# The values' product of two steps back directly behind the scores, in an attention stage that shares TensorE with experts

## The chip, the core and the metric

The kernel runs on one NeuronCore of a Trainium2 chip. Five engines work from their own instruction queues: TensorE (PE; its weight loads are listed apart as PEld), VectorE (DVE), ScalarE (ACT), GpSimd (POOL) and SyncE (SP, here only a queue that issues DMAs). They wait for each other by semaphores. The metric is device time in microseconds (us) of one execution. All data are float32.

## What is computed

The reference is a network of two layers on 8 x 512 tokens of width 256. The first layer (a state-space block and a mixture of eight experts) is not touched by the change. The second layer is an attention block plus a mixture of experts, both on the same normalised rows:

```python
xn = _layernorm(x, axis=-1)
x = x + _L1_attn_ref(xn, ...) + _L1_ffn_ref(xn, ...)

# attention: 16 heads of 16, batch 8, sequence 512
scores = jnp.einsum('bhqd,bhkd->bhqk', qh, kh) * scale
scores = scores * decay[None, None, :, :]
attn = jax.nn.softmax(scores, axis=-1)
out = jnp.einsum('bhqk,bhkd->bhqd', attn, vh)

# experts: seven experts with 512 rows each, and one that passes its rows on
h = jax.nn.relu(jnp.einsum('ceh,ehi->cei', inputs, experts_inter))   # 256 -> 1024
out = jnp.einsum('cei,eih->ceh', h, experts_out) * in_w[..., None]   # 1024 -> 256
combined = jnp.zeros_like(x_flat).at[used_idx].add(out.reshape(-1, hidden))
```

## The kernel before

All engines run the instructions in the order in which the program issues them (a schedule written by hand). The first layer takes roughly the first 1100 us. Behind it comes the loop over attention steps, in which everything named here happens.

An attention step covers one batch `b`, one group `g` of four heads and one block `c` of 128 keys, against all 512 queries: 8 x 4 x 4 = 128 steps. A step's work is spread over three rounds of the loop:

- `scores` (L1554): four matmuls, one for each head, contracting over 16 rows. The heads lie at partitions 0, 32, 64 and 96, so that the four run beside each other in four row groups of the array; each writes a bank of its own, of four (`s_ps`). VectorE multiplies each with the decay, takes the maximum and writes the result `s` (L1564), then makes `ng` and `w` from the maxima (L1569, L1571).
- one round later: `shares` (L1573, a small exponential of `w`), `exps((0, 1))` and `exps((2, 3))` (L1576: the exponentials of two heads each, in place, on ACT) and `weigh` (L1580: VectorE scales the values by `w` into `wv`).
- two rounds later: `values` (L1584): four matmuls that contract over the 128 keys and write 32 partitions each of one bank `o_ps`, so that the four run beside each other in four column groups. They need `wv` and the four exponentials. After the fourth block of keys (`c == 3`) `divide` (L1651) copies `o_ps` to `os` on ACT and stores it to DRAM by SP.

A float32 matmul is recorded as two MATMUL instructions, so that a step has eight for the scores and eight for the values.

Between these, `fill()` (L1729) issues one piece of other work on the whole 128 x 128 array. It takes the first of: a piece that is half done, urgent work, and the experts, the last only while fewer of their pieces are spent than `due()` (L1713) asks for at this step. In the first steps it takes late work of the layer before instead. The pieces of the experts come from `experts()` (L1383). For each half of an expert (256 rows) there are 17:

- one piece that transposes the rows (`e_tp`, L1399) and has ACT copy them (`e_xdT`, L1400)
- eight of the first layer (`e_hp`, L1407: four MATMUL instructions each), each followed on ACT by a ReLU (`e_hT`, L1410)
- eight of the second layer (`e_yp`, L1420: four MATMUL instructions each), in two groups of four that, once begun, go on at every `fill()`; behind the fourth of a group ACT scales the result (`e_yo`, L1426) and POOL adds it to rows in DRAM (L1427)

All of them write to two banks in turn. Urgent work is the output projection of a finished batch (`finish`, L1517: four pieces `fin`, each with a copy on ACT and an addition on VectorE), and, at the end, the last batch's own steps.

A round has up to four pieces. In what follows they are A, B, C and D: A behind `exps((0, 1))` and ahead of the values, B behind the values, then `exps((2, 3))` and `weigh`, then C and D. On TensorE only the scores, the values and the pieces appear; on ACT the exponentials stand between the pieces' own copies and ReLUs.

Of the kernel before, what the change touches and what calls it, by code (L numbers as in the profile page):

```python
# [63 lines left out]
def tile_kernel(ctx: ExitStack, tc: tile.TileContext, t, out: bass.AP):  # L64
# [505 lines left out]
    with ExitStack() as es:  # L570
# [648 lines left out]
        with tc.manual_schedule(engines=ENGINES):  # L1219
# [62 lines left out]
            def fill(n):  # L1282
                for _ in range(n):
                    if next(rows, "end") == "end":
                        next(rest, None)
# [73 lines left out]
    with tc.tile_pool(name="a1", bufs=1) as p1, tc.tile_pool(name="a2", bufs=2) as p2, tc.tile_pool(  # L1359
# [89 lines left out]
        def load_some(k):  # L1449
            for to, of in loads[:k]:  # L1450
                Y.dma_start(out=to, in_=of)
            del loads[:k]

        def inputs_of(b):
            rows, vd = kept[b]
            got = {"q": [], "k": [], "v": p2.tile([P, TPB, VW], FP, name="vt", tag="vt")}
            Y.dma_start(out=got["v"], in_=vd)
            for n in ("q", "k"):
                spread(rows[n], got[n], n)
            return got  # L1460
# [26 lines left out]
        class Ending:  # L1487
# [11 lines left out]
            def divide(self):  # L1499
                tq = psum.tile([P, 2, P], FP, name="tq", tag="s_ps", bufs=4)  # L1500
                T.transpose(tq[:, 0, :], self.os[:, self.at], ident)
                T.transpose(tq[:, 1, :], self.last, ident)
                self.oq = columns(tq)
# [188 lines left out]
        with tc.manual_schedule(engines=ENGINES):  # L1692
# [53 lines left out]
            def more():  # L1746
                if spent == WORK:
                    next(rows, None)

            def follow():  # L1750

                nonlocal work, ready, e1, e2
                if late_left:
                    pass
                elif ready is None:
                    ready = n
                    tls.close()
                    e1 = es.enter_context(tc.tile_pool(name="f1", bufs=1, side="right"))
                    e2 = es.enter_context(tc.tile_pool(name="f2", bufs=2, side="right"))
                    work = experts()  # L1760
                    next(work)
                elif n == ready + 1:
                    next(work)

            def own_rows(b):
                Y.dma_start(out=x_sb[:, b * TPB : (b + 1) * TPB, :], in_=rows_of(xn1, b))
# [4 lines left out]
            for n in range(N + 2):  # L1771

                if n < N:
                    b, g, c = steps[n]
                    if (g, c) == (2, 0) and b + 1 < B:
                        got = inputs_of(b + 1)
                    if (g, c) == (1, 0) and b < B - 1:
                        own_rows(b)
                        if b == B - 2:
                            own_rows(B - 1)  # L1780
                    if b == B - 1 and g == 0:
                        xi = x_sb[:, b * TPB + c, :]
                        V.tensor_scalar(xi, xi, noop[:, b * TPB + c : b * TPB + c + 1], None, ALU.mult)
                    if (g, c) == (0, 0):
                        now_in = got
                        od = dram.tile([4, 4, 32, S], FP, name="od", tag="od", bufs=2)
                        rd = dram.tile([AH, S], FP, name="rd", tag="rd", bufs=2)
                        scratch = (od, rd, [])
                    now = Step(b, g, c, now_in)
                    now.scratch = scratch  # L1790
                    done.append(now)
                    now.scores()
                load_some(6)
                for chain in list(chains):
                    if next(chain, "end") == "end":
                        chains.remove(chain)
                if ready is not None and n == ready + 3:
                    idle.append(work)
                last = done[n - 1] if 1 <= n <= N else None
                if last:  # L1800
                    last.shares()
                    last.exps((0, 1))
                    fill()
                m = n - 2
                if m >= 0:
                    s = done[m]
                    if s.c == 0:
                        s_op = psum.tile([P, S], FP, name="o_ps", tag="o_ps", bufs=2)
                    s.values(s_op)
                    if s.c == TPB - 1:  # L1810
                        if m == N - 1:
                            tails = [Ending(s.b, c, s_op, s.scratch[2]) for c in range(TPB)]
                        else:
                            chains.append(divide(s.b, s.g, s_op, *s.scratch))
                            next(chains[-1], None)
                if last:
                    fill() or more()
                    last.exps((2, 3))
                    last.weigh()
                    fill()  # L1820
                    fill() or more()
                    if late_left:
                        fill()
                follow()
# [77 lines left out]
def build(arrays):  # L1902
    import concourse.bacc as bacc

    nc = bacc.Bacc("TRN2", target_bir_lowering=False, num_devices=1)
    t = {
        k: nc.dram_tensor(f"in_{k}_dram", v.shape, mybir.dt.from_np(v.dtype), kind="ExternalInput").ap()
        for k, v in arrays.items()
    }
    out = nc.dram_tensor("out_0_dram", (NT, DM), FP, kind="ExternalOutput").ap()  # L1910
    with tile.TileContext(nc) as tc:
        tile_kernel(tc, t, out)
    return nc
# [10 lines left out]
```

## Time and profile before

| | |
|---|---|
| three runs, median (lowest to highest) | 1805.91 us (1796.79 to 1808.62) |
| the profiled execution | 1802.12 us, its span 1800.4 us |
| mean granted TensorE clock in the span | 0.913 of full speed |
| first scores, last values of the attention steps | 1137 us, 1784 us from the span's start |
| first and last piece of the experts' first layer | 1212 us, 1714 us |

The profile's page gives for each engine its busy time, and the groups of instructions with their idle time and what ended it. The ends of matmuls are modelled, so TensorE can be listed as busy while it waits; the distance from one start to the next tells more. In a timeline the columns are the start (us from the span's start), the duration from the first to the last instruction of the line (us), engine, line of the program, operation, what is written and read, shapes, and how many instructions are merged; in brackets the idle time before and what ended it.

### The profile page before, as it was taken

The page shows a single profiled execution, that of the slowest core. Times are in us where ns is not written, and L with a number is a line of the kernel's source. Part 1 is how long each engine was busy: PE and PEld are TensorE (multiplying, and loading weights), DVE is VectorE, ACT ScalarE, POOL GpSimd, SP SyncE. Part 2 cuts the span into 40 slices and gives each one's busy share as a digit, 9 for nine tenths or more (in the row PEclk, how much of TensorE's full clock was granted, in tenths as well). Part 3 has the DMA queues.
Part 4 walks back from the last instruction along what each step waited for, and adds up shares of the span by engine and source line. Part 5 has one row for each costly group of instructions (what it writes and reads, how often), then busy time and mean ns, then how long its engine had stood idle before and what let it go on. Part 6 is the DMA issues. An engine that isn't in the chain of part 4 may idle for free.

```text
span 1800.4 us, 25907 instructions
## 1 busy us (share of the span) xinstructions
PE 1630.7 (91%) x8736; PEld 980.5 (54%) x8736; DVE 1201.4 (67%) x3166; ACT 914.8 (51%) x2173; POOL 574.7 (32%) x520
## 2 busy tenths in 40 slices
PE   6556889989999999998798889879999999999997
PEld 6224567667677776775455556444544545444442
DVE  6578586575765765757877575566667666666674
ACT  4232344454454544544544523337767676766674
POOL 0041465475574654754323220001112111211030
PEclk8777799999999999999898898759999999999996
DMA  8010544554475445642644433232433324334163
GB/s 298 6 53 7 168 158 172 188 176 156 155 234 182 159 176 177 208 146 86 145 147 131 124 85 111 91 114 63 126 92 105 116 60 128 87 110 125 48 102 112
DMA packets 131789, 230.56 MB, mean 128 GB/s; under 512 B 20093, under 2 KB 93823, under 8 KB 120512
## 3 DMA queue, kind: packets, MB, share of 16 engines
q1 hardware_dynamic: 101952, 119.46, 21.4%
q0 software_dynamic: 28656, 108.69, 19.8%
q8 instruction: 73, 1.20, 0.3%
q10 hardware_dynamic: 1040, 0.66, 0.1%
q14 instruction: 68, 0.56, 0.1%
HBM read 176.23 MB, written 53.05 MB: 127 GB/s over the span
## 4 chain that ended last, share of the span: by engine, by line
PE 44%; DVE 6%; ACT 1%; issue 1%; DMA 0%; SPq 0%; POOL 0%; DVEq 0%; ACTq 0%
PE s_ps L1561 10%; PE o_ps L1586 8%; PE e_hp L1407 7%; PE e_yp L1420 6%; PE fin L1521 2%; PE qp L265 2%; PE pj L939 2%; PE tab L230 1%; PE pp L765 1%; DVE s L1564 1%; PE op L1084 1%; PE seg L1127 1%; PE yd L1165 1%; PE lp L250 1%; PE e_tp L1399 1%
## 5 line engine op out<-in xcount | busy, mean ns | idle before, releaser
L1564 DVE CUSTOM_DVE_ANT_0 s<-s_ps,band 128x512 f32<-128x512 f32 x512 | 322.9, 687 | 183.0 <-PE s_ps L1561 179.9
L1578 ACT ACTIVATE s<-s,ng 128x512 f32<-128x512 f32 x512 | 335.6, 711 | 0.0
L939 PE MATMUL pj<-xT,w_w_in 128*128 128x512 f32 x384 | 198.5, 643 | 11.7 <-DVE cv L952 7.5
L1561 PE MATMUL s_ps<-qT,kT 16*128 16x512 f32 x1024 | 198.7, 694 | 4.5 <-DMA kT<-kd 4.5
L1427 POOL DMA_INDIRECT x<-e_yo,number x28 | 44.7, 1597 | 445.7 <-ACT w L1574 291.0
L952 DVE SCALAR_TENSOR_TENSOR cv<-pj,w_conv_w,cv 128x511 f32<-128x511 f32 (+2 forms) x192 | 143.1, 746 | 20.5 <-ACT cv L948 16.0
L1111 POOL TENSOR_TENSOR au<-da,half 128x512 f32<-128x512 f32 x64 | 77.6, 1213 | 245.1 <-PE seg L1127 174.2
L1586 PE MATMUL o_ps<-s,wv 128*32 128x512 f32 x1024 | 154.5, 677 | 0.9 <-ACT w L1574 0.9
L642 PEld LDWEIGHTS h_ps<-xdT,w 128*128 128x128 f32 x1152 | 138.9, 194 | 21.3 <-issue 20.5
L642 PE MATMUL h_ps<-xdT,w 128*128 128x128 f32 x1152 | 142.1, 277 | 2.6 <-DMA w<-in_w_dram,w_idx 2.6
L666 PE MATMUL y_ps<-w,hT 128*128 128x256 f32 x576 | 137.9, 383 | 0.0
L1407 PEld LDWEIGHTS e_hp<-e_xdT,e_w 128*128 128x128 f32 x448 | 77.9, 191 | 87.3 <-issue 39.3
L666 PEld LDWEIGHTS y_ps<-w,hT 128*128 128x128 f32 x576 | 108.1, 193 | 29.8 <-issue 16.1
L1407 PE MATMUL e_hp<-e_xdT,e_w 128*128 128x256 f32 x448 | 124.2, 405 | 0.0
L939 PEld LDWEIGHTS pj<-xT,w_w_in 128*128 128x128 f32 x384 | 70.2, 201 | 92.8 <-issue 80.6
L1561 PEld LDWEIGHTS s_ps<-qT,kT 16*128 16x128 f32 x1024 | 66.5, 196 | 86.2 <-DVE peaks L1564 42.9
L1420 PE MATMUL e_yp<-e_w,e_hT 128*128 128x256 f32 x448 | 112.6, 394 | 0.0
L1420 PEld LDWEIGHTS e_yp<-e_w,e_hT 128*128 128x128 f32 x448 | 81.0, 191 | 54.1 <-issue 37.6
L1140 ACT ACTIVATE mt<-seg,mid 64x64 f32<-64x64 f32 x512 | 109.7, 309 | 0.8
L1174 DVE TENSOR_TENSOR yT<-yT,yd 128x512 f32<-128x512 f32 (+1 forms) x64 | 43.7, 683 | 98.0 <-PE yd L1165 97.0
L956 ACT ACTIVATE th<-cv 128x512 f32<-128x512 f32 x64 | 40.3, 630 | 120.1 <-DVE cv L952 107.4
L1159 DVE TENSOR_TENSOR mt<-mt,cbm 128x1024 f32<-128x1024 f32 x64 | 96.5, 1508 | 0.1
(340 smaller groups left out, 2819.8 us busy)
## 6 DMA issues: line engine op xcount, KB each, us to landing
ex<-exd SPq DMA_DIRECT2D x96, 128.0 KB
fr<-fdd SPq DMA_DIRECT2D x64, 128.0 KB
od<-os SPq DMA_DIRECT2D x28, 256.0 KB
e_w<-in_ei_dram SPq DMA_DIRECT2D x7, 1024.0 KB
e_w<-in_eo_dram SPq DMA_DIRECT2D x7, 1024.0 KB
vd<-vt SPq DMA_DIRECT2D x16, 272.0 KB
vt<-vd SPq DMA_DIRECT2D x8, 544.0 KB
u<-in_u_dram SPq DMA_DIRECT2D x8, 512.0 KB
```

The lines of the kernel that those rows point to most:

```text
L642: T.matmul(hp[:, i, :], w1[:, k * FF + f * P : k * FF + (f + 1) * P], xdT[:, k * P : (k + 1) * P], start=(k == 0), stop=(k == KC - 1),)
L666: T.matmul(yp, hT[f // 4][:, f % 4, :], w2[:, f * DM : (f + 1) * DM], start=(f == 0), stop=(f == FC - 1),)
L939: T.matmul(pj, w_in[:, k, o * P : (o + 1) * P], self.xT[:, k, :], start=(k == 0), stop=(k == KC - 1))
L952: V.scalar_tensor_tensor(cv[:, s:], pj[:, : S - s], conv_w[:, q, 3 - s : 4 - s], cv[:, s:], ALU.mult, ALU.add)
L1140: A.activation(mt[lo, over, h], seg[lo, over, h], AF.Exp, bias=mid[lo, self.i, h : h + 1])
L1159: V.tensor_tensor(self.mt, self.mt, bc(self.cbm, 1, H3), ALU.mult)
L1407: T.matmul(hp, w1[:, k, f * P : (f + 1) * P], xdT[:, k, :], start=(k == 0), stop=(k == KC - 1))
L1420: T.matmul(yp, hT[:, f, c * P : (c + 1) * P], w2[:, f, :], start=(f == 0), stop=(f == FC - 1))
L1561: T.matmul(sp[i], self.k[r, cols], self.q[r, :], start=True, stop=True)
L1564: V.tensor_tensor_reduce(out=self.p[i], in0=sp[i], in1=band[:, at : at + S], scale=1.0, scalar=KEEP, op0=ALU.mult, op1=ALU.max, accum_out= ...
L1578: A.activation(self.p[i], self.p[i], AF.Exp, bias=self.ng[:, i : i + 1])
L1586: T.matmul(op[32 * i : 32 * i + 32, :], self.wv[:, i, :], self.p[i], start=(self.c == 0), stop=(self.c == TPB - 1),)
```

## The change

In each round the first `fill()` moves from its place behind `exps((0, 1))` to a place behind the values' product and, where a group ends, the first stage of `divide`. The other pieces, `exps((2, 3))` and `weigh` keep their places.

```diff
@@ -1800,7 +1800,6 @@
                 if last:
                     last.shares()
                     last.exps((0, 1))
-                    fill()
                 m = n - 2
                 if m >= 0:
                     s = done[m]
@@ -1814,6 +1813,7 @@
                             chains.append(divide(s.b, s.g, s_op, *s.scratch))
                             next(chains[-1], None)
                 if last:
+                    fill()
                     fill() or more()
                     last.exps((2, 3))
                     last.weigh()
```

On TensorE a round was: scores, A, values, B, C, D. It becomes: scores, values, A, B, C, D. On ACT a round was: `shares`, two exponentials, A's work, the copy of a finished group, B's work, two exponentials, the work of C and D. It becomes the same with the copy of a finished group ahead of A's work. On SP the store of that copy moves ahead of what A issues. The numbers of pieces per round, which `due()` sets by the step's number, are as before. Once, in the last batch, the piece that `divide` puts ahead of all others (L1658 and the lines behind it) is put there before the round's first `fill()` and not after it.

## The prediction

> **What bounds it now.** I read the page first, then the stage by windows, then the order of work within single steps.
>
> ```profile
> PE 1630.7 (91%) x8736; PEld 980.5 (54%) x8736; DVE 1201.4 (67%) x3166; ACT 914.8 (51%) x2173; POOL 574.7 (32%) x520
> PE 44%; DVE 6%; ACT 1%; issue 1%; DMA 0%; SPq 0%; POOL 0%; DVEq 0%; ACTq 0%
> ```
>
> From the page: TensorE is busy 91% of the span and carries most of the chain of waits that is attributed. Both lines average over stages, so the windows come next (columns: span, then PE, PEld, DVE, ACT, POOL busy, granted clock, DMA share, GB/s).
>
> ```profile
> 1388.00:1398.00 10.00, 10.00 (x49) 3.75 (x48) 5.72 (x22) 5.85 (x12) 3.73 (x3) 0.83 0.21 42
> 1500.00:1550.00 50.00, 50.00 (x282) 24.19 (x280) 33.28 (x122) 35.19 (x75) 9.47 (x7) 1.00 0.35 99
> ```
>
> In the stage that the diff touches TensorE is 100% busy by the model, ACT 70%, VectorE 67%. "Busy" hides waits there, as the timeline of TensorE shows:
>
> ```profile
> 1491.47 1.14 PE L1561 MATMUL s_ps<-qT,kT 16*128 16x512 f32 x8
> 1492.54 1.07 PE L1586 MATMUL o_ps<-s,wv 128*32 128x512 f32 x8
> 1493.54 2.80 PE L1561 MATMUL s_ps<-qT,kT 16*128 16x512 f32 x8
> 1496.27 1.13 PE L1420 MATMUL e_yp<-e_w,e_hT 128*128 128x256 f32 x4
> 1497.33 1.07 PE L1586 MATMUL o_ps<-s,wv 128*32 128x512 f32 x8
> 1498.33 2.86 PE L1420 MATMUL e_yp<-e_w,e_hT 128*128 128x256 f32 x12
> 1501.11 0.71 PE L1561 MATMUL s_ps<-qT,kT 16*128 16x512 f32 x4
> ```
>
> I read prices from start to start. Scores cost 1.07 us whether the values' product follows (1491.47 to 1492.54) or a piece does; values cost 1.00 whether scores follow (1492.54 to 1493.54) or a piece does (1497.33 to 1498.33). One piece alone costs 1.06 (1496.27 to 1497.33), three in a row 2.78, so a further piece costs (2.78-1.06)/2 = 0.86, and 0.20 of each run of pieces is the change of shape. The scores at 1493.54 take 2.73: their banks come free only as VectorE reduces the step before.
>
> ```profile
> 1515.79 1.14 PE L1561 MATMUL s_ps<-qT,kT 16*128 16x512 f32 x8
> 1515.90 0.38 ACT L1410 ACTIVATE e_hT<-e_hp 128x256 f32<-128x256 f32 x1 [1.59 <-PE e_hp L1407]
> 1516.18 1.32 ACT L1578 ACTIVATE s<-s,ng 128x512 f32<-128x512 f32 x2
> 1516.86 1.13 PE L1407 MATMUL e_hp<-e_xdT,e_w 128*128 128x256 f32 x4
> 1517.41 0.19 ACT L1574 ACTIVATE w<-w 128x4 f32<-128x4 f32 x1
> 1517.50 1.32 ACT L1578 ACTIVATE s<-s,ng 128x512 f32<-128x512 f32 x2
> 1517.92 1.06 PE L1586 MATMUL o_ps<-s,wv 128*32 128x512 f32 x8
> 1518.73 0.36 ACT L1410 ACTIVATE e_hT<-e_hp 128x256 f32<-128x256 f32 x1
> 1518.92 1.13 PE L1407 MATMUL e_hp<-e_xdT,e_w 128*128 128x256 f32 x4
> ```
>
> This is the commonest step (the next scores start at 1519.98, so it lasts 4.19). It has two first-layer pieces, A at 1516.86 ahead of the values and B at 1518.92 behind them. ACT's order is what matters: the ReLU of the step before's piece B (1515.90) stands ahead of the second pair of exponentials (1516.18 to 1517.50), and the values at 1517.92 need that pair. Now they start 0.42 after it, thanks to piece A.
>
> ```profile
> 1507.03 1.14 PE L1561 MATMUL s_ps<-qT,kT 16*128 16x512 f32 x8
> 1508.10 0.66 PE L1399 MATMUL e_tp<-ident,e_xd 128*128 128x128 f32 x4
> 1508.68 1.06 PE L1586 MATMUL o_ps<-s,wv 128*32 128x512 f32 x8
> 1508.79 0.59 ACT L1400 COPY e_xdT<-e_tp 128x512 f32<-128x512 f32 x1
> 1509.68 1.99 PE L1407 MATMUL e_hp<-e_xdT,e_w 128*128 128x256 f32 x8
> ```
>
> A transposing piece: the values hide ACT's copy (1508.79 to 1509.38) that the next piece needs.
>
> **The change, part by part.** Nothing is added or removed; the values' eight matmuls (and at a group's end the copy of their result on ACT and its store on SP) move ahead of piece A. Along TensorE's timeline from 1207 to 1740 I counted the steps by the pieces before and behind the values: 34 with one ReLU piece on each side; 22 with one and three second-layer pieces; 7 with one and three projections; 7 with one and two ReLU pieces; 6 with one ReLU and three second-layer pieces; 10 with a transposing piece and one to three ReLU pieces behind (five of these have just one); 6 with a lone second-layer piece; the rest have a lone transposing piece or none.
>
> *Gain.* 34+22+7+7+6 = 76 steps have plain pieces on both sides and lose one change of shape: 76 x 0.20 = 15.2 us saved.
>
> *New wait at the values.* Count from the start of the scores. The second exponentials end at 1517.50 - 1515.79 = 1.71, and are released by piece B of the step before, which moves with the scores. The values would start at 1.07. The fourth head's share needs the last exponential. Does it matter that three heads can go ahead? The nearest row is the delayed scores: their last bank was freed at 1495.16 (VectorE's row there: the fourth reduction's end) and the next operation started at 1496.27, 1.11 later, so a last head alone takes as long as all four (1.07). So I count the whole delay: 1.71 + about 0.05 for the semaphore - 1.07 = 0.69, less 0.01 for the fourth head's own offset, 0.68. Behind the values on TensorE's queue wait all pieces, and behind the pieces the next scores; the next step's exponentials wait again for piece B, so the delay repeats every step: 1.76 + 1.00 + 1.06 + 0.86 = 4.67 instead of 4.19. It strikes after each step whose last piece is a ReLU in slot B: 34 + 5 = 39 times, 39 x 0.68 = 26.5 us lost. From both sides: 0 if the values could wait without cost, 39 x 0.74 = 29 if the four heads start together after the wait. Where a third piece follows B (12 steps of the kinds with two or three pieces behind) its ReLU and the exponentials are done 0.86 earlier, at 0.85, and nothing waits; with second-layer pieces in B and C ACT has nothing in between.
>
> *Transposing steps.* Values at 1.07, transposes at 2.07, copy done 1.28 later (1508.10 to 1509.38), plus 0.05: the ReLU piece starts at 3.41, not at 2.65. 10 x 0.76 = 7.6 us lost; the cover that was there, the values, is gone.
>
> *A lone second-layer piece* ends at the next scores instead of 1.0 earlier, so its scaling (about 0.4 on ACT) delays the exponentials; those scores wait for VectorE until 4.80 in any case (1491.47 to 1496.27), and I get about 0.2 beyond it: 6 x 0.2 = 1.2 us.
>
> *Nothing for:* the copy of the values' result, which now stands ahead of piece A's ReLU on ACT (0.59, done well before piece A ends, since A starts only when the values end; without that cover 0.6 in 28 steps); SP's store of it, which passes only a weight load needed some twenty microseconds later; POOL's scatters, which start at most 1 us later beside a POOL that is mostly idle. VectorE's order does not change. Before 1207 and after 1740 reductions, routing and half clock set the pace; I allow -4 to +4 and take 0.
>
> *The clock.* In the 10 us around 1393 the granted clock is 0.83, that is 10 x 0.17 = 1.7 us lost, after one wait of 1.67 us in the scores (2.73 for 1.07); six waits of 0.60 (scores at 1306.88 take 1.67) had no such dip. The new waits are of 0.7, so I add nothing. [...]
>
> **Sum:** -15.2 + 26.5 + 7.6 + 1.2 = +20.1 us. The profiled execution took 1802.12 (span 1800.4 and 1.7 around it), 3.8 below the median 1805.91: 1822.2 against its own time, 1826 against the median.
>
> **Rivals.**
> 1. *The wait is half hidden* (0.2). If the last head alone costs half of the 0.99 and the first three overlap the wait, 39 x 0.18 = 7 remains: -15.2+7+7.6+1.2 = +0.6, 1806.5. The delayed scores above speak against it, but they wait for their output's banks, not for an operand.
> 2. *No wait, faster than before* (0.1). If the second exponentials are done by 1.07 from the scores' start (piece B's ReLU would have to be released 0.69 earlier), the sum is -15.2+7.6 = -7.6, 1798. ACT has 1.0 idle in a 4.19 step, which speaks for it; but that idle time lies ahead of B's ReLU, waiting for it, which speaks against. Even with the transposing steps free the gain would be 15 us, under 1%.
> 3. *The clock follows* (0.1). If waits of 0.7 in successive steps bring one dip in each of the 14 half-experts, 14 x 1.7 = 24 on top: 1850. Against: the six waits of 0.6.
> The forecast has 0.6.
>
> **How the numbers follow.** About 1% (18 us) is what a measurement here can tell from no change. Forecast 1826, its own range 1817 to 1835 (0.62 to 0.74 for the wait, 4 us for head and tail). Slower by over 1%: two thirds or more of the forecast's share, given that 20.1 is just above 18, the clock case, and what other costs at nothing may add: 0.57. Faster by over 1% needs more than the whole gain: 0.05. Within 1%: 0.38. The range takes in rival 1 and part of rival 3: 1804 to 1840.
>
> **What would show it.** Values directly behind scores in the TensorE timeline, steps with two ReLU pieces at 4.67; idle time before the values' weight loads released by ACT's exponentials, some 39 times; four second-layer pieces in 3.64 instead of 3.84; 1.34 between transposes and the next piece. I am wrong if two-piece steps take 3.99 (no wait), or if the granted clock over 1210 to 1740 falls clearly below its 0.98.

## The result, and the profile after

| | before | after |
|---|---|---|
| median of ten runs each (lowest to highest) | 1799.38 us (1785.08 to 1815.06) | 1821.48 us (1807.41 to 1830.94) |
| ratio to before, 95% interval | | 1.0131, 1.0098 to 1.0164 |
| span of the profiled execution | 1800.4 us | 1819.1 us |

The change made the kernel slower by 1.3% (17.6 to 29.5 us by the interval). The ratio is taken over the executions in the faster of two states that the kernel's runs show, so it is not quite the ratio of the two medians. From the page of the changed kernel, the lines that answer to the two first ones of before:

```profile
PE 1646.6 (91%) x8736; PEld 998.8 (55%) x8736; DVE 1200.6 (66%) x3166; ACT 917.0 (50%) x2173; POOL 576.0 (32%) x520
PE 77%; DVE 16%; ACT 3%; issue 2%; DMA 2%; POOL 0%; SPq 0%; ACTq 0%; DVEq 0%; POOLq 0%
```

The same instructions on every engine. TensorE is "busy" 16 us longer, most of the difference, though it does not one matmul more: waits within a group of matmuls count as busy (the values' eight are listed with 1.74 in steps with a wait below, with 1.06 without). (The shares of the chain can't be compared with those of before, where only some 52% of the span was attributed.) The windows by stage, first of the kernel before, then of the changed one, cut in both at the first scores, the first scores that share their round with experts, the first scores behind the last projection, and the end (columns as in the windows above):

```profile
1137.21:1207.69 70.48, 58.29 (x221) 31.12 (x221) 46.84 (x188) 25.75 (x50) 4.40 (x5) 0.57 0.31 98
1207.69:1740.79 533.10, 533.10 (x2845) 255.85 (x2841) 348.30 (x1296) 366.93 (x764) 78.25 (x59) 0.97 0.34 95
1740.79:1800.42 59.63, 47.64 (x203) 15.66 (x202) 34.27 (x136) 30.76 (x66) 9.95 (x11) 0.68 0.57 132
```

```profile
1140.68:1210.17 69.49, 58.52 (x220) 31.58 (x220) 47.08 (x187) 25.80 (x50) 4.41 (x5) 0.57 0.32 100
1210.17:1760.96 550.79, 544.04 (x2844) 271.63 (x2840) 348.13 (x1296) 369.00 (x764) 76.60 (x58) 0.98 0.32 91
1760.96:1819.13 58.17, 46.79 (x203) 15.60 (x202) 34.21 (x136) 30.77 (x66) 11.59 (x12) 0.71 0.62 141
```

Of the 18.7 us between the two spans, 3.5 lie ahead of the first scores, in code that the change doesn't touch; the early steps give -1.0, the end -1.5; the stage with the experts gives +17.7. TensorE's timeline there, in the changed kernel:

```profile
1217.78 1.14 PE L1561 MATMUL s_ps<-qT,kT 16*128 16x512 f32 x8
1218.85 1.06 PE L1586 MATMUL o_ps<-s,wv 128*32 128x512 f32 x8
1219.84 1.99 PE L1407 MATMUL e_hp<-e_xdT,e_w 128*128 128x256 f32 x8
1221.77 1.14 PE L1561 MATMUL s_ps<-qT,kT 16*128 16x512 f32 x8
1222.84 1.74 PE L1586 MATMUL o_ps<-s,wv 128*32 128x512 f32 x8
1224.50 1.99 PE L1407 MATMUL e_hp<-e_xdT,e_w 128*128 128x256 f32 x8
1226.43 1.14 PE L1561 MATMUL s_ps<-qT,kT 16*128 16x512 f32 x8
...
1232.16 1.74 PE L1586 MATMUL o_ps<-s,wv 128*32 128x512 f32 x8
1233.82 3.72 PE L1420 MATMUL e_yp<-e_w,e_hT 128*128 128x256 f32 x16
1237.47 0.71 PE L1561 MATMUL s_ps<-qT,kT 16*128 16x512 f32 x4
```

The first of these steps follows one without a late ReLU: values 0.99 us (1218.85 to 1219.84), step 3.99, 0.20 less than the 4.19 of before. From then on the values take 1.66 (1222.84 to 1224.50) and the step 4.66. Four second-layer pieces take 3.65 (1233.82 to 1237.47) instead of 1.06 + 2.78. What the values wait for shows in all engines' timeline of the second step:

```profile
1221.87 0.38 ACT L1410 ACTIVATE e_hT<-e_hp 128x256 f32<-128x256 f32 x1 [0.48 <-PE e_hp L1407]
1222.15 1.32 ACT L1578 ACTIVATE s<-s,ng 128x512 f32<-128x512 f32 x2
1222.84 0.22 PEld L1586 LDWEIGHTS o_ps<-s,wv 128*32 128x32 f32 x6 [0.76 <-ACT e_hT L1410]
1222.84 1.74 PE L1586 MATMUL o_ps<-s,wv 128*32 128x512 f32 x8
1223.53 0.14 PEld L1586 LDWEIGHTS o_ps<-s,wv 128*32 128x32 f32 x2 [0.47 <-ACT s L1578]
```

Six of the eight weight loads, those of three heads, go at once; the last two, of the fourth head, start at 1223.53, released by ACT's exponentials, which end at 1222.15 + 1.32 = 1223.47. The next piece starts 0.97 after that, at 1224.50. Distances of 1.66 to 1.68 from the values to what follows occur 40 times in the stage; the kernel before has two between 1.6 and 1.7, both at half clock. And a transposing step:

```profile
1363.85 1.14 PE L1561 MATMUL s_ps<-qT,kT 16*128 16x512 f32 x8
1364.92 1.06 PE L1586 MATMUL o_ps<-s,wv 128*32 128x512 f32 x8
1365.91 0.66 PE L1399 MATMUL e_tp<-ident,e_xd 128*128 128x128 f32 x4
1366.61 0.59 ACT L1400 COPY e_xdT<-e_tp 128x512 f32<-128x512 f32 x1 [0.92 <-PE e_tp L1399]
1367.25 1.13 PE L1407 MATMUL e_hp<-e_xdT,e_w 128*128 128x256 f32 x4 [0.68 <-ACT e_xdT L1400]
1368.31 0.31 PEld L1561 LDWEIGHTS s_ps<-qT,kT 16*128 16x128 f32 x8 [0.33 <-DVE wv L1582]
```

TensorE stands idle 0.68 for the copy that the values used to hide: the ReLU piece starts 3.40 behind the scores, and the step takes 4.46; the same step took 3.72 before.

### The profile page after: what moved, and what is told of

It is laid out like the page before. It is cut to its first block, busy times and chain, and to the rows that moved or that the text cites. A ratio compares the mean times of both kernels' runs of the same rounds, so it can differ in the third digit from the quotient of the medians.

```text
span 1819.1 us, 25942 instructions
## 1 busy us (share of the span) xinstructions
PE 1646.6 (91%) x8736; PEld 998.8 (55%) x8736; DVE 1200.6 (66%) x3166; ACT 917.0 (50%) x2173; POOL 576.0 (32%) x520
## 4 chain that ended last, share of the span: by engine, by line
PE 77%; DVE 16%; ACT 3%; issue 2%; DMA 2%; POOL 0%; SPq 0%; ACTq 0%; DVEq 0%; POOLq 0%
PE s_ps L1561 10%; PE o_ps L1586 9%; PE pj L939 8%; PE h_ps L642 6%; PE y_ps L666 6%; PE e_hp L1407 6%; PE e_yp L1420 6%; PE yd L1165 3%; DVE cv L952 3%; PE seg L1127 3%; PE op L1084 3%; PE sp L1195 2%; PE yoff L1183 2%; PE qp L265 2%; PE tab L230 2%
## 5 line engine op out<-in xcount | busy, mean ns | idle before, releaser
L939 PE MATMUL pj<-xT,w_w_in 128*128 128x512 f32 x384 | 203.7, 658 | 11.0 <-DVE cv L952 6.7
L1586 PE MATMUL o_ps<-s,wv 128*32 128x512 f32 x1024 | 178.8, 662 | 1.4 <-issue 0.9
L642 PEld LDWEIGHTS h_ps<-xdT,w 128*128 128x128 f32 x1152 | 139.0, 194 | 20.7 <-issue 19.9
L1407 PE MATMUL e_hp<-e_xdT,e_w 128*128 128x256 f32 x448 | 111.9, 392 | 6.8 <-ACT e_xdT L1400 6.8
L1420 PEld LDWEIGHTS e_yp<-e_w,e_hT 128*128 128x128 f32 x448 | 86.2, 198 | 36.5 <-issue 24.4
L1586 PEld LDWEIGHTS o_ps<-s,wv 128*32 128x32 f32 x1024 | 30.6, 112 | 128.7 <-ACT s L1578 43.9
```

The source lines that it names most:

```text
L642: T.matmul(hp[:, i, :], w1[:, k * FF + f * P : k * FF + (f + 1) * P], xdT[:, k * P : (k + 1) * P], start=(k == 0), stop=(k == KC - 1),)
L939: T.matmul(pj, w_in[:, k, o * P : (o + 1) * P], self.xT[:, k, :], start=(k == 0), stop=(k == KC - 1))
L1407: T.matmul(hp, w1[:, k, f * P : (f + 1) * P], xdT[:, k, :], start=(k == 0), stop=(k == KC - 1))
L1420: T.matmul(yp, hT[:, f, c * P : (c + 1) * P], w2[:, f, :], start=(f == 0), stop=(f == FC - 1))
L1586: T.matmul(op[32 * i : 32 * i + 32, :], self.wv[:, i, :], self.p[i], start=(self.c == 0), stop=(self.c == TPB - 1),)
```

## The experiments

The whole time of one execution scatters by some 1.5% between lowest and highest, and the start of the first scores alone lies anywhere from 1127 to 1141 us in the profiles below. So each run is read twice: by its ratio to the kernel before (twelve runs each, ten of the changed kernel itself, six of the changed kernel with the ReLU issued twice), and by the length of its expert stage in its profile, cut as above. TensorE's granted clock falls to half there in some windows of 3.41 us, as the trace records it (the changed kernel's first from 1242.65 to 1246.07, with a granted clock of 0.50). Their number differs from profile to profile, and one costs some 1.64 us, so it is given beside. The windows of two steps of the same form in the changed kernel show the price, 9.02 against 7.38 at a mean granted clock of 0.81 against 1.00:

```profile
1705.85:1713.23 7.38, 7.38 (x36) 4.28 (x33) 5.21 (x22) 3.71 (x7) 0.42 (x1) 1.00 0.35 71
1512.05:1521.07 9.02, 9.02 (x37) 5.48 (x33) 5.51 (x21) 4.30 (x8) 0.42 (x1) 0.81 0.67 217
```

| kernel | ratio, 95% interval | stage, us | against before | windows at half clock |
|---|---|---|---|---|
| before | 1 | 533.1 | | 7 |
| changed | 1.0131 (1.0098 to 1.0164) | 550.8 | +17.7 | 5 |
| changed, exponentials first | 0.9914 (0.9881 to 0.9947) | 523.1 | -10.0 | 5 |
| before, exponentials first | 1.0021 (0.9989 to 1.0052) | 536.7 | +3.6 | 5 |
| changed, transposes ahead | 1.0037 (1.0001 to 1.0073) | 550.3 | +17.2 | 8 |
| both mended | 0.9919 (0.9884 to 0.9954) | 522.1 | -11.0 | 6 |
| changed, ReLU twice | 1.0193 (1.0153 to 1.0233) | 570.7 | +37.6 | 6 |
| before, ReLU twice | 1.0005 (0.9973 to 1.0038) | 536.0 | +2.9 | 6 |
| both mended, all transposes | 0.9905 (0.9868 to 0.9942) | 523.3 | -9.8 | 10 |
| changed, one exponential late | 0.9957 (0.9924 to 0.9991) | 529.4 | -3.7 | 8 |

**The wait taken away.** The theory: the loss is ACT's order, the values wait for exponentials behind piece B's ReLU. The rival: the new order is dear on TensorE itself.

```diff
                     last.exps((0, 1))
+                    last.exps((2, 3))
...
                     fill() or more()
-                    last.exps((2, 3))
```

> Changed kernel, with ACT's second pair of exponentials issued directly behind the first pair, ahead of the pieces' copies and ReLUs. My theory (the values wait for exponentials that stand behind piece B's ReLU): the 39 waits go, two-piece ReLU steps last 3.99 us instead of 4.66, lone second-layer pieces cost nothing. The transposing steps stay dear, and a little dearer than in the changed kernel, since the copy now stands behind four exponentials: 10 x 0.9 to 1.0 us. Sum against before: -15.2 + 9 to 10 = about -6 us, ratio 0.997. Rival (values directly behind scores, or the long run of pieces, are dear on TensorE itself, by the change of the array's shape): nothing goes, ratio stays at 1.01, steps stay at 4.66.

TensorE's timeline in this kernel:

```profile
1225.97 1.14 PE L1561 MATMUL s_ps<-qT,kT 16*128 16x512 f32 x8
1227.04 1.06 PE L1586 MATMUL o_ps<-s,wv 128*32 128x512 f32 x8
1228.04 1.99 PE L1407 MATMUL e_hp<-e_xdT,e_w 128*128 128x256 f32 x8
1229.96 1.14 PE L1561 MATMUL s_ps<-qT,kT 16*128 16x512 f32 x8
```

The values take 1.00 again and the step 3.99, with TensorE's order the same as in the changed kernel. The rival falls: values directly behind scores are not dear. As expected the transposing pieces got dearer, 1.38 to 1.49 from transposes to the ReLU piece at full clock against 1.33. The ratio is better than the 0.997 that I expected, outside its interval. The stage has -10.0, of which two windows at half clock fewer account for 3.3; what is left, -6.7, is the -6 of the sum. The interval's near end is -9.6 us for the whole kernel. Part of the rest can be the clock: every run has a span and a mean granted clock on record, and span x (1 - clock), the most that full clock could have saved, is 147.9 us on average here and 154.1 in the kernel before, so up to 6.2 us. How much of that counted isn't shown.

**The control.** The same two lines moved in the kernel before.

> Kernel before, with only ACT's second pair of exponentials moved directly behind the first pair. A control for the run before this one. My theory: in the kernel before, piece A covers the exponentials with 0.42 us to spare, so nothing is gained; two-piece steps stay at 4.19; transposing steps may lose some tenths each because the copy stands behind four exponentials. Ratio 1.000 to 1.004. Rival (the order on ACT is worth something by itself): faster than before by several us, ratio 0.996 or lower.

Ratio 1.0021, two-piece steps at 4.19, and a transposing step with one ReLU piece went from 3.72 to 4.61 (in TensorE's timeline scores start at 1358.04, 1362.65 and 1366.84, 4.61 and 4.19 apart). The stage's +3.6, with two windows at half clock fewer, is a loss of 7 us, all of it in the ten transposing steps, whose copy now stands behind four exponentials. So with piece A between scores and values moving the exponentials forward gains nothing; it is worth the wait only where the values stand directly behind the scores.

**The cover of the transposes given back.** A flag says that the experts' next piece transposes; that piece stays ahead of the values.

```diff
                     last.exps((0, 1))
+                    turn_now = turning[0] and not half_done and not urgent and idle and spent < due()
+                    if turn_now:
+                        fill()
                 m = n - 2
...
                 if last:
-                    fill()
+                    if not turn_now:
+                        fill()
```

> Changed kernel, but a transposing piece stays ahead of the values as before; all other first pieces are behind them. My theory: only the ten transposing steps change, from 3.40 us between scores' start and the ReLU piece's start back to 2.65: 7.6 us less than the changed kernel, some +12 us against before, ratio 1.007; the 39 waits stay (steps at 4.66). Rival (the wait for the transposes' copy is hidden by some other wait, of ACT or VectorE, in the same step): same time as the changed kernel, ratio 1.011 to 1.013.

Only half of it was done: of the ten transposing pieces with a ReLU piece behind, five followed a projection whose entry still stood in `urgent`, and stayed behind the values. In TensorE's timeline of this kernel one that was moved:

```profile
1471.92 0.66 PE L1400 MATMUL e_tp<-ident,e_xd 128*128 128x128 f32 x4
1472.51 1.07 PE L1590 MATMUL o_ps<-s,wv 128*32 128x512 f32 x8
1473.50 1.99 PE L1409 MATMUL e_hp<-e_xdT,e_w 128*128 128x256 f32 x8
```

(The program's lines have moved by one to four in this kernel.) The ReLU piece starts 1.58 behind the transposes with the values between them, and the step took 6.24 against 6.98 in the changed kernel: 0.74 saved, as expected. Five times that, 3.7 us, is what the run can show. The stages differ by -0.5 with three windows at half clock more (4.9), the ratios, 1.0037 and 1.0131, by more than the steps explain; here too the clock took less, 144.8 us on average against 151.0 in the changed kernel by span x (1 - clock). So the size is read from the single steps, and the whole time agrees in direction only.

**Both mended.** The flag, and the second pair of exponentials behind the first pair (or, in a transposing step, behind the transposing piece's copy).

```diff
                     if turn_now:
                         fill()
+                    last.exps((2, 3))
...
                     fill() or more()
-                    last.exps((2, 3))
```

> Changed kernel with both mended: a transposing piece stays ahead of the values, and the second pair of exponentials stands ahead of piece B on ACT (directly behind the first pair, or behind the transposing piece's copy). My theory: only the gain is left, 76 x 0.20 = 15 us: ratio 0.9915 against before, two-piece steps 3.99 us, group steps 5.72. Rival (what is saved on TensorE is given back: with steps this short VectorE's reductions, or the step's other waits, take its place): ratio 0.995 to 1.000, steps longer than 3.99 or longer waits in the scores.

Ratio 0.9919, with half of the transposing steps mended. The stage, allowing for one window at half clock fewer, is 9.4 us shorter; expected were 15, and the five transposing steps that were not mended, in the order of the run with the exponentials first, still lose up to 0.9 each, an estimate from its 1.49 (1.07 + 0.99 + 1.49 + 1.06 = 4.61 where 3.72 stood). The steps keep 3.99 and 5.72, so nothing takes the waits' place: the scores' wait for VectorE sits where it sat, in the steps behind one without pieces or with a lone one (over the whole profile 45.2 us in 97 waits of at most 1.7, against 42.9 in 87 in the kernel before).

**The suspected cost made longer.** Each ReLU of the first layer issued twice, once in the changed kernel, once in the kernel before.

```diff
                         A.activation(hT[:, f, :], hp, AF.Relu)
+                        A.activation(hT[:, f, :], hp, AF.Relu)
```

> Changed kernel with every ReLU of the experts' first layer issued twice on ACT (the same result twice). This lengthens what stands ahead of the second pair of exponentials by 0.28 us and touches nothing on TensorE. My theory: each of the 39 waits of the values grows from 0.68 to 0.96, two-piece steps from 4.66 to 4.94; where a third ReLU piece follows, about 0.1 for 12 steps: +12 us over the changed kernel, about +31 against before, ratio 1.018. Rival (the loss of the changed kernel doesn't come from ACT's queue): same time as the changed kernel, ratio 1.011 to 1.013.

> Kernel before with every ReLU of the experts' first layer issued twice on ACT (the same result twice). My theory: the second pair of exponentials ends 0.28 us later, at 1.99 from the scores' start, and the values start at 2.13, so the slack of 0.42 takes it all: steps stay at 4.19, ratio 1.000. Rival (ACT's load, not the order, sets the pace): the same 0.28 x 39 to 0.28 x 100 = 11 to 28 us as in the changed kernel, ratio 1.006 or more.

From the timeline of the changed kernel with ReLU twice, ACT's rows and the values, behind scores that start at 1291.16:

```profile
1291.27 0.38 ACT L1410 ACTIVATE e_hT<-e_hp 128x256 f32<-128x256 f32 x1
1291.68 0.38 ACT L1411 ACTIVATE e_hT<-e_hp 128x256 f32<-128x256 f32 x1
1291.96 1.32 ACT L1579 ACTIVATE s<-s,ng 128x512 f32<-128x512 f32 x2
1292.23 2.15 PE L1587 MATMUL o_ps<-s,wv 128*32 128x512 f32 x8
```

The second ReLU, which writes the same tile, costs 0.41 from start to start, not the 0.28 that I had taken from a ReLU with an exponential behind it. The values' distance to the next piece is 2.08 or 2.09 in 38 steps, 0.42 more than the 1.67: the lengthening is passed on one to one. Expected were 0.28; with 0.41 the sum is 39 x 0.41 = 16 us over the changed kernel, and the stage shows 19.9 with one window at half clock more (1.64), so 18.3. Most of the rest lies in the nine steps with three ReLU pieces in a row, each of which is 0.3 longer beyond the wait (6.24 against 5.52 in the commonest form). In the kernel before the same lengthening does nearly nothing in the commonest step, as TensorE's timeline there shows:

```profile
1513.44 1.14 PE L1562 MATMUL s_ps<-qT,kT 16*128 16x512 f32 x8
1514.51 1.13 PE L1407 MATMUL e_hp<-e_xdT,e_w 128*128 128x256 f32 x4
1515.57 1.09 PE L1587 MATMUL o_ps<-s,wv 128*32 128x512 f32 x8
1516.59 1.13 PE L1407 MATMUL e_hp<-e_xdT,e_w 128*128 128x256 f32 x4
1517.65 1.14 PE L1562 MATMUL s_ps<-qT,kT 16*128 16x512 f32 x8
```

The step takes 4.21 instead of 4.19: the slack of 0.42 is spent (ACT's row has the pair from 1514.24 for 1.32, to 1515.56, and the values start at 1515.57), and the values just begin to wait (1.02 for 1.00). Over the stage it costs 4.5 us (2.9, and one window at half clock fewer), about 2.4 of it in the steps with two or three ReLU pieces behind the values; the ratio is 1.0005. The same work on ACT costs 18.3 us in one order and 4.5 in the other: the load on ACT alone does not make the loss, its place does.

**The wait made shorter.** Three exponentials first, one behind piece B.

```diff
-                    last.exps((0, 1))
+                    last.exps((0, 1, 2))
...
-                    last.exps((2, 3))
+                    last.exps((3,))
```

> Changed kernel with three of the four exponentials issued directly behind each other and only the fourth behind piece B's ReLU. This halves what stands ahead of the last exponential's end: it ends 0.38 + 0.71 = 1.10 us from the scores' start, with the semaphore 1.15, where the fourth head would start at 1.09. My theory (the delay of the last head is passed on in full and nothing else is): the values' 39 waits shrink from 0.68 to 0.06, two-piece steps last 4.05; transposing steps about as in the changed kernel, 3.4 to 3.5 to the ReLU piece: -15.2 + 39 x 0.06 + 8 to 9 = about -4 us against before, ratio 0.997. Rival (a wait of any length on ACT costs a stall of about half a microsecond or more): two-piece steps above 4.3, ratio 1.003 or more.

TensorE's timeline:

```profile
1249.04 1.14 PE L1561 MATMUL s_ps<-qT,kT 16*128 16x512 f32 x8
1250.11 1.13 PE L1586 MATMUL o_ps<-s,wv 128*32 128x512 f32 x8
1251.16 1.99 PE L1407 MATMUL e_hp<-e_xdT,e_w 128*128 128x256 f32 x8
1253.09 1.14 PE L1561 MATMUL s_ps<-qT,kT 16*128 16x512 f32 x8
```

Steps of 4.05, and the values at 1.06 in 37 places. The stage has -3.7 with one window at half clock more, so -5.3 where -4 were expected. The kernels with all four exponentials first, one late, two late, and two late behind a doubled ReLU line up: the values take 0, 0.06, 0.67 and 1.09 us longer, where ACT's order makes the fourth head late by 0, 0.06, 0.67 and 0.67 + 0.41. The delay of the last head is the whole of the wait.

**All transposing pieces ahead.** As both mended, with the flag's test passing a projection that has given its last piece.

```diff
-turning[0] and not half_done and not urgent and idle and spent < due()
+turning[0] and not half_done and (over[0] or not urgent) and idle and spent < due()
```

> As the run with both mended, but with the transposing pieces that follow a projection put ahead of the values too (there, half of the ten were not, since the projection's queue was not yet closed). My theory: five more steps save 0.76 to 0.9 us, 4 us less than that run: 15 us less than before, ratio 0.991, two-piece steps 3.99, transposing steps with one ReLU piece 3.72. Rival (no more is to be had here, other waits take the place): same as that run, 0.992 or more, with transposing steps above 3.72.

```profile
1354.59 1.14 PE L1566 MATMUL s_ps<-qT,kT 16*128 16x512 f32 x8
1355.66 0.66 PE L1400 MATMUL e_tp<-ident,e_xd 128*128 128x128 f32 x4
1356.25 1.06 PE L1591 MATMUL o_ps<-s,wv 128*32 128x512 f32 x8
1357.24 1.13 PE L1409 MATMUL e_hp<-e_xdT,e_w 128*128 128x256 f32 x4
1358.31 1.15 PE L1566 MATMUL s_ps<-qT,kT 16*128 16x512 f32 x8
```

In TensorE's timeline of this kernel such a step takes 3.72 again, two-piece steps 3.99. The profiled stage had ten windows at half clock against seven; less 1.64 for each, the stages are 506.9 and 521.6, 14.7 apart where 15 were expected. Ratio 0.9905: faster than both kernels by its interval; whether it beats the two simpler versions (0.9914, 0.9919) the runs cannot tell.

## Why the prediction was right

Forecast were 20.1 us on the kernel's own time, ratio 1.011; measured is 1.0131 (1.0098 to 1.0164). By the steps:

- *The gain* per step that joins pieces, 0.20: right. Where nothing waits, 4.19 became 3.99, 5.91 became 5.72, 5.05 became 4.85 (with the exponentials first).
- *The wait at the values*, 39 times 0.68: right, 40 places with 0.67 (one of them behind a lone transposing piece, which I had counted at nothing), and the runs with the wait gone, shortened and lengthened show that it is ACT's order that makes it and that it is passed on in full.
- *Transposing steps*, 0.76: 0.74 or 0.75 in six of the seven that ran at full clock in both kernels, and with these pieces back ahead of the values, in the last run, the loss is gone.
- *A lone second-layer piece*, 0.2: right, six places where the values take 1.16, 0.17 more.
- *Nothing* for the copy of the values' result, for the queues of SP and POOL and for head and tail: the two outer stages moved by -1.0 and -1.5, within the 4 us allowed. The copy and the queues were not tested apart; in the stage all the steps together leave next to nothing for them, as the sum below shows.
- *Rival 1*, the wait half hidden: the fourth head's two weight loads start when its exponential ends, and the next piece 0.97 behind. That three heads go ahead gains next to nothing: the values take 0.99 where nothing waits.
- *Rival 2*, no wait: what it describes came true only where the exponentials were moved too, with ratios of 0.9905 to 0.9919; their intervals hold the gain of 15 us that it named (0.9917).
- *Rival 3*, the clock: five windows at half clock against seven. All five begin within a step whose scores waited 1.7 for VectorE, none in the runs of steps with waits of 0.67.

The stage's +17.7 is the 20.1, less 3.3 for two half-clock windows fewer, and 0.9 more, of which 0.7 is the fortieth wait. That there were two windows fewer was not forecast, and from one profile of each kernel it can be chance. The time came out at 1821.48 and not at 1826 mainly because I set out from a median of three runs, 1805.91; over ten runs the kernel before has 1799.38. Two slips in the working change nothing: the terms of the two-piece step add to 4.68 where 4.67 stands (measured 4.66), and the two terms named for the forecast's own range give 6 us to either side, not the 9 of 1817 to 1835.

## What to carry to other kernels

Before work is moved away from between two dependent steps, look up when the operand of the second is ready on the other engine's own queue: here piece A was 1.06 us of cover over 0.69 us of need, and taking it away cost more than three times what the better order on TensorE saved in such a step. If the order is worth having, move the producer on its queue in the same edit. Where the whole time scatters by as much as the effect, lengths of like steps in the timeline, and a lengthened suspect in both orders, decide what the medians can't.

## What the runs showed that I had not expected

In these profiles the granted clock falls to half for one to three windows of 3.41 us that begin within a step whose scores waited some 1.7 us (three where the 20 us from 1390 of the changed kernel with ReLU twice have a mean clock of 0.74); behind the stage's first step no such window of the ten profiles begins elsewhere in the stage. Each profile has fifteen such steps, and in four to seven of them the clock falls. That makes five to ten windows in this stage, for kernels with nearly the same work, and a window costs some 1.64 us. What decides which of the fifteen bring a fall is not shown.

In the changed kernel with ReLU twice, two ReLUs in a row that write the same tile start 0.41 us apart (1291.27 to 1291.68), against 0.28 from a ReLU to an exponential of another tile (1291.68 to 1291.96).
